# The prologue of an AdaLN-FFN block kernel: first products ahead of the second pairs' convolutions, W_up loaded earlier, half of agg_w in another buffer

## The chip, the cores and the metric

The kernel runs on one core of one Trainium2 chip. The metric is the time of one execution on the device, in microseconds (us); the median of three runs is what counts. TensorE (PE in the profile) multiplies, VectorE (DVE) and GpSimd (POOL) do elementwise work, ScalarE (ACT) copies and activations, and SyncE (SP) issues DMA transfers; DMAs can also be issued by ACT and POOL. Each engine works through its own instructions in the order in which the program gives them, and the order is written out by hand here.

## The reference

A batch of 128 samples with 64 channels of 1,024 values goes through two blocks, each of which adds its result to x:

```
# block 0: a per-sample channel mix, then a low-rank layer
att   = softmax(mlp(cond_128))                      # 128 x 8
agg_w = einsum('bk,koi->boi', att, weight); agg_b = att @ bias_k
y     = einsum('boi,bih->boh', agg_w, x) + agg_b[:, :, None]
x     = x + y @ (A @ B.T).T + bias                  # rank 128
# block 1: grouped convolution (9 taps, 4 groups), then a routed layer
y     = conv1d(x, weight, groups=4) + ctx + fside
base  = y @ W_up.T                                  # 1024 x 1024
one   = one_hot(argmax(y @ gate_w.T + expert_bias)) # 4 experts
delta = sum over e of one[e] * (y @ lora_A[e].T) @ lora_B[e].T
x     = x + base + delta
```

## The kernel before

**Tiling.** Two samples make a *pair*: a tile of 128 partitions (2 x 64 channels) by 1,024. There are 64 pairs, and two pairs, 2d and 2d+1, make a *group* d of the last layer, 32 groups in all.

**Block 0 for a pair.** `layer0_in` multiplies the transposed x by B into the PSUM tile pxb, and ScalarE copies it to xb. `layer0_mix` multiplies xb by the pair's agg_w (pz, then z: pairs 0 to 3 have theirs from `own_bd` and `own_bias`, which VectorE and ScalarE compute in the kernel; later pairs read it back from the DRAM tile aggd through `load_cond`). `layer0_out` multiplies z by A (pd, two halves), VectorE adds it to x, SP writes x to a DRAM tile x1d and reads it back in the order that the convolution needs into one of three SBUF tiles X (pair number modulo 3). The read waits until the write has landed. `add_fbias` adds the bias to x on VectorE or GpSimd.

**Convolution for a pair.** Pairs 0 and 1 use `conv`: products of X with the taps (pc, L429), evacuated by VectorE into the tile yt. From pair 2 on it takes `differences` (GpSimd reads X), `shared_in` (pm, L400), `shared_out`, `conv_in` (pc, L438) and `conv_out`.

**The last layer for a group.** W_up is held in quarters 11, 12, 21, 22 of 1 MB each, and the product takes seven half-size products instead of eight, with the weights T1 = 12 - 11, T2 = 22 - T1, T3 = 22 - 12 and -T4 = 21 - T2 (`w_sum`, VectorE, once) and with sums s0 to s3 of y (`ffn_sums`, GpSimd). A group does `gate_in`, `ffn_a` (product with 11), `ffn_second` (21), then `ffn`: gate, T2, T3, T1, the transposition `turn`, -T4, 22. VectorE and GpSimd add the intermediate results u2 and u3 to x on the way; `tiles` runs the next group's convolution beside the low-rank products (`lora`) and stores the results.

**Order.** Lines 624 to 714 are the prologue: conditions, pairs 0 to 3 through block 0, the convolutions of pairs 0 to 3, block 0 of pair 4 and parts of pair 5, the first two products of group 0. From line 715 a loop over the 32 groups repeats one order; its first pass still has the five other products of group 0. `tiles(0)` begins with `shared_in(4)`.

**Queues and buffers.** SP's queue in the prologue has, in this order: x of pair 3, x1d and X of pair 1, W_11, W_21, x1d of pair 2, x of pair 4, X of pair 2, W_12 (four pieces, in the buffers of s0 to s3), W_22, x1d of pair 3, aggb and the two halves of agg_w to DRAM (`agg_out`), X of pair 3, and `load_cond(2)`, whose read of aggd waits until agg_w has landed. x of pairs 5 to 7 is issued by GpSimd. The two halves of agg_w wait in SBUF in the buffers that become T3 (wT3) and -T4 (w-T4); so `w_sum` for T3 and -T4 cannot write before agg_w has been stored.

Of the kernel before, what the change touches and what calls it, by code (L numbers as in the profile page):

```python
# [35 lines left out]
F32 = mybir.dt.float32  # L36
AF = mybir.ActivationFunctionType
ALU = mybir.AluOpType
# [3 lines left out]
P = 128  # L42
NB, CH, L = 128, 64, 1024
NPAIR = NB // 2
# [24 lines left out]
def block(ctx: ExitStack, tc: tile.TileContext, a: dict, out: bass.AP):  # L69
# [58 lines left out]
    load_x(0, nc.sync)  # L128
    at = loaded("AT", [P, L])
    wk = loaded("wk", [P, 8, 2, CH], eng=nc.scalar)  # L130
    W, W12 = {}, []

    def load_w(name, eng):
        W[name] = const.tile([P, HC, N], F32, name=f"w{name}")
        eng.dma_start(W[name], a[f"w{name}"])

    def load_w12(eng):
        for c in range(HC):
            W12.append(sums.tile([P, N], F32, tag=f"s{c}", name=f"w12_{c}"))
            eng.dma_start(W12[c], a["w12"][:, c])  # L140

    def w_sum(name, x, y):
        W[name] = const.tile([P, HC, N], F32, tag=f"w{name}", name=f"w{name}")
        if "12" not in (x, y):
            nc.vector.tensor_tensor(W[name], W[x], W[y], ALU.subtract)
            return
        for c in range(HC):
            u, w = (W12[c] if n == "12" else W[n][:, c] for n in (x, y))
            nc.vector.tensor_tensor(W[name][:, c], u, w, ALU.subtract)


    X = []
# [147 lines left out]
    def agg_all():  # L300

        to = aggd.rearrange("b i o -> b (i o)").rearrange("b (j h n) -> h b j n", j=4, h=2)
        for h in range(2):
            agg = const.tile([NB, 4, 512], F32, tag=("wT3", "w-T4")[h], name=f"agg{h}")
            aggs.append((to[h], agg))
            ps4 = [spare(j, f"pagg{h}_{j}") for j in range(4)]
            for j in range(4):
                rows = slice(32 * j, 32 * (j + 1))
                nc.tensor.matmul(ps4[j], attT[rows, :], wa[rows, h], start=True, stop=True)
            for j in range(4):  # L310
                if j % 2:
                    nc.scalar.copy(agg[:, j], ps4[j])
                else:
                    nc.vector.tensor_copy(agg[:, j], ps4[j])
            yield
# [5 lines left out]

    lo, hi = slice(0, N), slice(N, L)
    xbs, z0s, yts, opened = {}, {}, {}, {}
    diffs, pms, m2s, pcs, zgs, vs, ss = {}, {}, {}, {}, {}, {}, {}

    def layer0_in(pr):
        xt = xts.pop(pr)
# [20 lines left out]
            nc.vector.scalar_tensor_tensor(to, aggbs[g][:, t], bsum, pzv, ALU.mult, ALU.add)  # L348
        z0s[pr] = z0

    def layer0_out(pr, then=None):
        x, z0 = xs[pr], z0s.pop(pr)
        xt = X[pr % NX]
        d = x1d.tile([Q, P, P], F32, tag="x1d", name=f"x1d{pr}")
        dv = d.rearrange("q (c g) m -> (q c) g m", g=BG)
        h = P // 2
        for hf in range(2):
            cols = slice(hf * 512, (hf + 1) * 512)
            qs = slice(hf * Q // 2, (hf + 1) * Q // 2)
            pd = bank(f"pd{pr}_{hf}")  # L360
            nc.tensor.matmul(pd, z0, at[:, cols], start=True, stop=True)  # L361
            nc.vector.tensor_tensor(x[:, cols], pd, x[:, cols], ALU.add)  # L362
            nc.sync.dma_start(
                d[qs].rearrange("q r m -> r q m"), x[:, cols].rearrange("r (q m) -> r q m", m=P)
            )
        if then:
            then()
        nc.sync.dma_start(xt[h:, :, :P], dv[:h])
        nc.sync.dma_start(xt[:h, :, 1 : P + 1], dv[h:])

    def blocks(pr, b, g, first):

# [96 lines left out]
    def halves(d):  # L469

        yt = yts[d]
        return [[yt[:, t, h * HC : (h + 1) * HC] for h in range(2)] for t in range(2)]
# [36 lines left out]
    def gate(d):  # L509

        zg = zgs.pop(d)
        pt = bank(f"pgt{d}")
        for t in range(2):
            nc.tensor.matmul(pt[:, t * GL : (t + 1) * GL], zg[:, t], fold, start=True, stop=True)  # L514
        pv = pt[:, : 2 * GL].rearrange("p (t c) -> p t c", t=2)
        lg = sp.tile([P, 2, E], F32, tag="lg", name=f"lg{d}")
        nc.vector.tensor_tensor(lg, pv[:, :, :E], ebias.unsqueeze(1).to_broadcast([P, 2, E]), ALU.add)
        mx = sp.tile([P, 2], F32, tag="mx", name=f"mx{d}")
        nc.vector.tensor_reduce(mx, lg, AX.X, ALU.max)
        sc = sp.tile([P, 2, E], F32, tag="sc", name=f"sc{d}")  # L520
        nc.vector.tensor_tensor(sc, lg, mx.unsqueeze(2).to_broadcast([P, 2, E]), ALU.is_equal)
        nc.vector.tensor_tensor(sc, sc, rank.unsqueeze(1).to_broadcast([P, 2, E]), ALU.mult)
        ms = sp.tile([P, 2], F32, tag="ms", name=f"ms{d}")
        nc.vector.tensor_reduce(ms, sc, AX.X, ALU.max)
        oh = sp.tile([P, 2, E], F32, tag="oh", name=f"oh{d}")
        nc.vector.tensor_tensor(oh, sc, ms.unsqueeze(2).to_broadcast([P, 2, E]), ALU.is_equal)
        zm = sp.tile([P, 2, 2, E, R], F32, tag="zm", name=f"zm{d}")
        for h in range(2):
            nc.vector.tensor_tensor(
                zm[:, :, h],  # L530
                pv[:, :, E:].rearrange("p t (e r) -> p t e r", e=E),
                oh.unsqueeze(3).to_broadcast([P, 2, E, R]),
                ALU.mult,
            )
        return zm
# [8 lines left out]
    def ffn_second(d):  # L544
        product(opened[d][0], halves(d)[0][1], W["21"], False)

    def ffn(d):

        b1 = halves(d)[1][1]
        p, v, s = opened[d], vs.pop(d), ss.pop(d)  # L550
        xa, xb = xs[2 * d], xs[2 * d + 1]
        zm = gate(d)
        product(p[1], s[1], W["T2"])
        u2 = sums.tile([P, N], F32, tag="u2", name=f"u2_{d}")
        nc.vector.tensor_tensor(u2, p[1], v, ALU.add)  # L555
        nc.gpsimd.tensor_tensor(xa[:, hi], xa[:, hi], u2, ALU.add)  # L556
        nc.gpsimd.tensor_tensor(xb[:, lo], xb[:, lo], u2, ALU.add)
        if 2 * d + 4 < NPAIR:
            differences(2 * d + 4)
        product(p[2], s[2], W["T3"])  # L560
        u3 = sums.tile([P, N], F32, tag="u3", name=f"u3_{d}")
        nc.vector.tensor_tensor(u3, p[2], u2, ALU.add)
        nc.gpsimd.tensor_tensor(xb[:, hi], xb[:, hi], u3, ALU.add)
        if 2 * d + 5 < NPAIR:
            differences(2 * d + 5)
        product(p[3], s[0], W["T1"])
        nc.vector.tensor_tensor(xb[:, hi], p[3], xb[:, hi], ALU.add)  # L567
        zt = turn(d, zm)
        product(p[2], b1, W["-T4"], False)
        product(p[3], s[3], W["22"], False)  # L570
        del yts[d]
        return zt

    def lora(d, zt):

# [82 lines left out]
    load_context(1)  # L658
    gl = loaded("gl", [P, NC, GT], eng=nc.scalar)
    lb = loaded("lb", [P, N], eng=nc.scalar)  # L660
    layer0_out(1)
    load_w("11", nc.sync)
    load_w("21", nc.sync)
    wsum = const.tile([P, NGC, P], F32, tag="sel", name="wsum")
    nc.gpsimd.tensor_tensor(wsum, ws[:, :, 0], ws[:, :, 1], ALU.add)
    add_fbias(3, nc.gpsimd)
    next(agg)
    own_bd(2)
    own_bias(2)
    layer0_in(2)  # L670
    conv(0)
    layer0_mix(2)
    layer0_out(2, lambda: load_x(4, nc.sync))
    own_bd(3)
    own_bias(3)
    load_w12(nc.sync)
    load_w("22", nc.sync)
    layer0_in(3)
    conv(1)
    layer0_mix(3)  # L680
    layer0_out(3, agg_out)
    add_fbias(4, nc.gpsimd)
    differences(2)
    gate_out(0, gate_in(0))
    ffn_a(0)
    w_sum("T1", "12", "11")
    w_sum("T2", "22", "T1")
    load_x(5)
    load_cond(2)
    layer0_in(4)  # L690
    differences(3)
    ffn_second(0)
    shared_in(2)
    shared_in(3)
    conv_in(2, 0)
    shared_out(2)
# [5 lines left out]
    conv_out(2, 1)  # L702
    conv_out(3, 0)
    conv_out(3, 1)
    add_fbias(5, nc.gpsimd)
    layer0_in(5)
    layer0_mix(4)
    w_sum("T3", "22", "12")
    w_sum("-T4", "21", "T2")
    ffn_sums(0)  # L710
    layer0_mix(5)
    layer0_out(4)
    load_x(6)
    load_x(7)
    for d in range(NPAIR // 2):
        more = d + 1 < NPAIR // 2
        ahead = [pr for pr in (2 * d + 6, 2 * d + 7) if pr < NPAIR]
        if 2 * d + 5 < NPAIR:
            layer0_out(2 * d + 5)
            load_context(d + 2)  # L720
        if ahead:
            load_cond(d + 3)
        for pr in ahead:
            add_fbias(pr, nc.gpsimd)
        tiles(d, ffn(d), 2 * d + 4, 2 * d + 5)
        for pr in (2 * d + 8, 2 * d + 9):
            if pr < NPAIR:
                load_x(pr)
        if more:
            ffn_sums(d + 1)  # L730
        for pr in ahead:
            layer0_in(pr)
        if ahead:
            layer0_mix(ahead[0])
        if more:
            ffn_a(d + 1)
        if ahead:
            layer0_out(ahead[0])
            layer0_mix(ahead[1])
        if more:  # L740
            ffn_second(d + 1)
# [104 lines left out]
```

## Time and profile before

| | us |
|---|---|
| median of 3 runs | 1358.75 (1358.67 to 1359.2) |
| the profiled execution, run time | 1359.87 |
| its span, first to last instruction | 1358.0 |
| TensorE busy | 1322.0 (97%) |
| GpSimd busy | 614.9 (45%) |
| VectorE busy | 555.3 (41%) |
| ScalarE busy | 139.2 (10%) |
| chain of work that ended last: TensorE / DMA / VectorE | 93% / 4% / 2% |
| one pass of the loop (start of `shared_in` at 113.39 and 153.82 on the chain) | 40.43 |

The profile is that of one execution. The chain is followed back from the last instruction, at each step to what released it. "busy" of TensorE is the time in which a matmul is under way. PEclk is the share of full speed that the chip granted to TensorE. In the view by stretches each row is a window of the span; the columns are its length, then for each engine busy time and number of instructions, the granted clock, the mean busy share of the 16 DMA engines, and GB/s.

### The profile page before, as it was taken

The numbers are of one execution on the slowest core, as the hardware profiler recorded it, in microseconds if no ns is written. First come the engines' busy times: TensorE is split into PE (matmuls) and PEld (weight loads), VectorE is DVE, ScalarE is ACT, GpSimd is POOL, SyncE is SP. The second block draws the span as 40 slices with busy tenths as digits, with TensorE's granted clock in tenths as the row PEclk, the third lists the DMA queues.
The fourth block names the chain that finished last, engine by engine and source line by source line (L and its number), as shares of the span: only waits on it lengthen the run. The fifth ranks groups of instructions, "written<-read, shape, count | busy, mean of one in ns | idle before, by whom it ended". The sixth has DMA issues, their size and how long they took to land.

```text
span 1358.0 us, 18275 instructions
## 1 busy us (share of the span) xinstructions
PE 1322.0 (97%) x7303; PEld 762.2 (56%) x7303; DVE 555.3 (41%) x984; ACT 139.2 (10%) x310; POOL 614.9 (45%) x547
## 2 busy tenths in 40 slices
PE   8679999999999999999999999999999999999997
PEld 6445555566555566555566555556555556655543
DVE  6453443444342444343444343344344344444222
ACT  2101100011101011111011111011111011110000
POOL 2155345544345544435553435553435554346321
PEclk9979999999999999999999999999999999999999
DMA  8934445553445544445544434554444555343301
GB/s 295 325 103 148 119 119 165 151 156 126 125 108 159 158 146 144 125 112 140 165 149 140 133 105 134 165 150 144 130 108 129 165 151 154 118 124 99 96 32 62
DMA packets 184276, 189.37 MB, mean 139 GB/s; under 512 B 17408, under 2 KB 156672, under 8 KB 183808
## 3 DMA queue, kind: packets, MB, share of 16 engines
q1 hardware_dynamic: 166048, 122.66, 32.5%
q0 software_dynamic: 16992, 61.87, 13.7%
q10 hardware_dynamic: 1152, 3.67, 0.8%
q8 instruction: 58, 0.95, 0.3%
q14 instruction: 26, 0.21, 0.1%
HBM read 118.90 MB, written 69.27 MB: 139 GB/s over the span
## 4 chain that ended last, share of the span: by engine, by line
PE 93%; DMA 4%; DVE 2%; issue 0%; ACT 0%; SPq 0%; DVEq 0%; ACTq 0%
PE pb L465 56%; PE pxb L330 8%; PE pc L438 8%; PE pd L361 8%; PE pm L400 4%; PE pg L496 4%; PE pb L580 2%; DMA x1d<-x 2%; DMA X<-x1d 1%; PE pz L340 1%; PE pgt L514 1%; DMA x<-in_x 1%; DMA xt<-in_xt 0%; PE pc L429 0%; PE pzt L539 0%
## 5 line engine op out<-in xcount | busy, mean ns | idle before, releaser
L465 PE MATMUL pb<-wT,s 128*128 128x512 f32 x768 | 337.5, 596 | 0.0
L109 POOL DMA_DIRECT2D x<-in_x x59 | 31.1, 528 | 503.5 <-DVE z L348 417.8
L465 PEld LDWEIGHTS pb<-wT,s 128*128 128x128 f32 x768 | 143.6, 190 | 168.4 <-issue 168.1
L465 PE MATMUL pb<-w,yt 128*128 128x512 f32 x512 | 230.8, 593 | 3.1 <-DVE x L586 1.7
L362 DVE TENSOR_TENSOR x<-pd,x 128x512 f32<-128x512 f32 x128 | 88.3, 691 | 233.0 <-PE pd L361 232.8
L415 DVE TENSOR_TENSOR m<-pm,cx 64x512 f32<-64x512 f32 x124 | 85.4, 689 | 228.6 <-PE pm L400 225.7
L591 POOL TENSOR_TENSOR x<-x,ffn_bias 128x1024 f32<-128x1024 f32 x62 | 144.7, 2355 | 47.4 <-DMA x<-in_x 47.4
L465 PEld LDWEIGHTS pb<-w,yt 128*128 128x128 f32 x512 | 92.4, 190 | 98.6 <-issue 92.2
L330 PEld LDWEIGHTS pxb<-B,xt 128*128 128x128 f32 x1024 | 118.8, 194 | 24.6 <-DVE yt L450 22.0
L361 PE MATMUL pd<-AT,z 128*128 128x512 f32 x256 | 122.9, 602 | 7.9 <-DVE z L348 6.1
L450 DVE TENSOR_TENSOR yt<-pc,m 128x512 f32<-128x512 f32 x124 | 121.4, 1098 | 21.7 <-ACT m L418 20.8
L330 PE MATMUL pxb<-B,xt 128*128 128x128 f32 x1024 | 125.0, 280 | 0.0
L465 PE MATMUL pb<-w,s 128*128 128x512 f32 x256 | 116.9, 600 | 2.1 <-DVE x L567 2.1
L438 PE MATMUL pc<-ws,df 128*64 128x128 f32 x1984 | 115.3, 275 | 0.0
L465 PE MATMUL pb<-w-T,yt 128*128 128x512 f32 x256 | 115.2, 592 | 0.0
L438 PEld LDWEIGHTS pc<-ws,df 128*64 128x64 f32 x1984 | 112.2, 139 | 4.3
L418 ACT COPY m<-m 64x512 f32<-64x512 f32 x124 | 76.5, 617 | 282.8 <-DVE m L415 279.4
L556 POOL TENSOR_TENSOR x<-x,u 128x512 f32<-128x512 f32 x32 | 40.4, 1264 | 140.9 <-DVE u L555 140.9
L361 PEld LDWEIGHTS pd<-AT,z 128*128 128x128 f32 x256 | 48.6, 192 | 68.5 <-issue 58.4
L465 PEld LDWEIGHTS pb<-w,s 128*128 128x128 f32 x256 | 49.1, 192 | 64.8 <-issue 61.9
L465 PEld LDWEIGHTS pb<-w-T,yt 128*128 128x128 f32 x256 | 46.1, 190 | 55.1 <-issue 55.1
L400 PEld LDWEIGHTS pm<-wsum,X 128*64 128x64 f32 x992 | 54.4, 140 | 36.6 <-issue 36.6
(110 smaller groups left out, 1139.4 us busy)
## 6 DMA issues: line engine op xcount, KB each, us to landing
x1d<-x SPq DMA_DIRECT2D x128, 256.0 KB, 3.5
X<-x1d SPq DMA_DIRECT2D x128, 256.0 KB, 4.0
out<-x SPq DMA_DIRECT2D x64, 512.0 KB, 2.6
xt<-in_xt POOLq DMA_DIRECT2D x59, 512.0 KB, 4.5
x<-in_x POOLq DMA_DIRECT2D x59, 512.0 KB, 4.3
cx<-ctxd SPq DMA_DIRECT2D x32, 128.0 KB, 4.3
ab<-aggbd SPq DMA_DIRECT2D x30, 128.0 KB, 3.2
w<-in_w SPq DMA_DIRECT2D x3, 1024.0 KB, 8.9
```

Source lines behind the costliest of these rows:

```text
L330: nc.tensor.matmul(pxb[:, :P], xt[:, c, :], bt[:, c, :], start=(c == 0), stop=(c == NC - 1))
L361: nc.tensor.matmul(pd, z0, at[:, cols], start=True, stop=True)
L362: nc.vector.tensor_tensor(x[:, cols], pd, x[:, cols], ALU.add)
L400: nc.tensor.matmul(pm[b * H : (b + 1) * H, g * P : (g + 1) * P], blocks(pr, b, g, 1), wsum[:, g], start=True, stop=True,)
L415: nc.vector.tensor_tensor(by_group(m2[half, b]), by_group(pm[half]), context(pr, b, half), ALU.add)
L418: nc.scalar.copy(m2[other, b], m2[half, b])
L438: nc.tensor.matmul(pc[o * H : (o + 1) * H, cols], diffs[pr][:, 2 * g + b, o], ws[:, g, o], start=True, stop=True,)
L450: nc.vector.tensor_tensor(yt.rearrange("m q (o g two) -> m two g q o", two=2, g=NGC)[:, b], by_group(pcs.pop((pr, b))), context(pr, b) if ...
L465: nc.tensor.matmul(to, yt[:, c], w[:, c], start=first and c == 0, stop=c == HC - 1, skip_group_check=not first)
L496: nc.tensor.matmul(pg[rows, : 2 * P].rearrange("m (t r) -> m t r", t=2), gl[:, c, :], yt[:, :, c], start=c < 2, stop=c >= NC - 2,)
L556: nc.gpsimd.tensor_tensor(xa[:, hi], xa[:, hi], u2, ALU.add)
L591: eng.tensor_tensor(xs[pr], xs[pr], fbias, ALU.add)
```

## The change

The prologue and the first pass of the loop are put in another order; nothing is computed differently.

- `ffn` is cut into `ffn_both` (T2), `ffn_b` (T3), `ffn_hi` (T1) and `ffn_last` (turn, -T4, 22), so that the prologue can issue the parts of group 0 between other work. `layer0_out` can hand back its X reads (`later=True`) so that they are issued later.
- The second half of agg_w waits in a buffer of the pool of yt instead of that of -T4; W_12 is loaded whole into the buffer of -T4 instead of in four pieces into those of s0 to s3.
- W_11, W_21, W_12 and W_22, x of pair 4 and `agg_out` are issued ahead of x1d of pairs 2 and 3. W_11 is even ahead of X of pair 1. `load_cond(2)` stands ahead of X of pair 2. x of pairs 5 to 7 moves from GpSimd's queue to SP's.
- Block 0 of pairs 2 and 3 stands ahead of the convolution of pair 1; all products of group 0 up to T1 stand ahead of the convolutions of pairs 2 and 3, with block 0 of pairs 4 and 5 between them. -T4 and 22 come after these convolutions.

```diff
-            agg = const.tile([NB, 4, 512], F32, tag=("wT3", "w-T4")[h], name=f"agg{h}")
+            pool, tag = ((const, "wT3"), (ytp, "yt"))[h]
+            agg = pool.tile([NB, 4, 512], F32, tag=tag, name=f"agg{h}")
...
+        def back():
+            nc.sync.dma_start(xt[h:, :, :P], dv[:h])
+            nc.sync.dma_start(xt[:h, :, 1 : P + 1], dv[h:])
+        if later:
+            return back
+        back()
...
+    def ffn_both(d):
+        xa, xb = xs[2 * d], xs[2 * d + 1]
+        product(opened[d][1], ss[d][1], W["T2"])
+        u2s[d] = sums.tile([P, N], F32, tag="u2", name=f"u2_{d}")
+        nc.vector.tensor_tensor(u2s[d], opened[d][1], vs.pop(d), ALU.add)
+        nc.gpsimd.tensor_tensor(xa[:, hi], xa[:, hi], u2s[d], ALU.add)
+        nc.gpsimd.tensor_tensor(xb[:, lo], xb[:, lo], u2s[d], ALU.add)
+    def ffn_b(d):
+        xb = xs[2 * d + 1]
+        product(opened[d][2], ss[d][2], W["T3"])
+        u3 = sums.tile([P, N], F32, tag="u3", name=f"u3_{d}")
+        nc.vector.tensor_tensor(u3, opened[d][2], u2s.pop(d), ALU.add)
+        nc.gpsimd.tensor_tensor(xb[:, hi], xb[:, hi], u3, ALU.add)
+    def ffn_hi(d):
+        xb = xs[2 * d + 1]
+        product(opened[d][3], ss[d][0], W["T1"])
+        nc.vector.tensor_tensor(xb[:, hi], opened[d][3], xb[:, hi], ALU.add)
+    def ffn_last(d, zm):
+        p, s = opened[d], ss.pop(d)
         zt = turn(d, zm)
-        product(p[2], b1, W["-T4"], False)
+        product(p[2], halves(d)[1][1], W["-T4"], False)
         product(p[3], s[3], W["22"], False)
...
-    layer0_out(1)
-    load_w("11", nc.sync)
+    layer0_out(1, lambda: load_w("11", nc.sync))
+    load_x(4, nc.sync)
     load_w("21", nc.sync)
+    load_w("12", nc.sync, tag="w-T4")
+    load_w("22", nc.sync)
...
     next(agg)
+    agg_out()
     own_bd(2)
     own_bias(2)
     layer0_in(2)
+    own_bd(3)
+    own_bias(3)
     conv(0)
     layer0_mix(2)
-    layer0_out(2, lambda: load_x(4, nc.sync))
-    own_bd(3)
-    own_bias(3)
-    load_w12(nc.sync)
-    load_w("22", nc.sync)
+    back2 = layer0_out(2, later=True)
     layer0_in(3)
+    layer0_mix(3)
+    back3 = layer0_out(3, later=True)
+    load_cond(2)
+    back2()
+    load_x(5, nc.sync)
+    back3()
     conv(1)
-    layer0_mix(3)
-    layer0_out(3, agg_out)
+
+    gate_out(0, gate_in(0))
+    ffn_sums(0)
     add_fbias(4, nc.gpsimd)
-    differences(2)
-    gate_out(0, gate_in(0))
     ffn_a(0)
+    layer0_in(4)
     w_sum("T1", "12", "11")
     w_sum("T2", "22", "T1")
-    load_x(5)
-    load_cond(2)
-    layer0_in(4)
+    w_sum("T3", "22", "12")
+    ffn_second(0)
+    zm = gate(0)
+    ffn_both(0)
+    ffn_b(0)
+    differences(2)
+    layer0_mix(4)
+    layer0_out(4, lambda: load_x(6, nc.sync))
+    w_sum("-T4", "21", "T2")
+    ffn_hi(0)
+    add_fbias(5, nc.gpsimd)
     differences(3)
-    ffn_second(0)
+    layer0_in(5)
+    layer0_mix(5)
+    back5 = layer0_out(5, lambda: load_x(7, nc.sync), later=True)
     shared_in(2)
+    back5()
     shared_in(3)
     conv_in(2, 0)
...
-    add_fbias(5, nc.gpsimd)
-    layer0_in(5)
-    layer0_mix(4)
-    w_sum("T3", "22", "12")
-    w_sum("-T4", "21", "T2")
-    ffn_sums(0)
-    layer0_mix(5)
-    layer0_out(4)
-    load_x(6)
-    load_x(7)
     for d in range(NPAIR // 2):
...
+        if d and 2 * d + 5 < NPAIR:
+            layer0_out(2 * d + 5)
         if 2 * d + 5 < NPAIR:
-            layer0_out(2 * d + 5)
             load_context(d + 2)
...
-        tiles(d, ffn(d), 2 * d + 4, 2 * d + 5)
+        if d:
+            zt = ffn(d)
+        else:
+            differences(4)
+            differences(5)
+            zt = ffn_last(0, zm)
+        tiles(d, zt, 2 * d + 4, 2 * d + 5)
```

More of the change, by code (lines that the diff above doesn't have):

```diff
@@ L130, in block, with load_w @@
     wk = loaded("wk", [P, 8, 2, CH], eng=nc.scalar)
-    W, W12 = {}, []
-    def load_w(name, eng):
-        W[name] = const.tile([P, HC, N], F32, name=f"w{name}")
+    W = {}
+    def load_w(name, eng, tag=None):
+        W[name] = const.tile([P, HC, N], F32, tag=tag or f"w{name}", name=f"w{name}")
         eng.dma_start(W[name], a[f"w{name}"])
[L137 to L140, printed above, removed]
     def w_sum(name, x, y):
         W[name] = const.tile([P, HC, N], F32, tag=f"w{name}", name=f"w{name}")
[L144 to L149, printed above, removed]
+        nc.vector.tensor_tensor(W[name], W[x], W[y], ALU.subtract)
     X = []
@@ L323, in block @@
     xbs, z0s, yts, opened = {}, {}, {}, {}
-    diffs, pms, m2s, pcs, zgs, vs, ss = {}, {}, {}, {}, {}, {}, {}
+    diffs, pms, m2s, pcs, zgs, vs, ss, u2s = {}, {}, {}, {}, {}, {}, {}, {}
     def layer0_in(pr):
@@ L349, in layer0_mix, with layer0_out @@
         z0s[pr] = z0
-    def layer0_out(pr, then=None):
+    def layer0_out(pr, then=None, later=False):
         x, z0 = xs[pr], z0s.pop(pr)
@@ L367, in layer0_out @@
             then()
-        nc.sync.dma_start(xt[h:, :, :P], dv[:h])
-        nc.sync.dma_start(xt[:h, :, 1 : P + 1], dv[h:])
+        def back():
[4 more added lines that the diff above has]
+        back()
     def blocks(pr, b, g, first):
@@ L545, in ffn_second @@
         product(opened[d][0], halves(d)[0][1], W["21"], False)
-    def ffn(d):
-        b1 = halves(d)[1][1]
-        p, v, s = opened[d], vs.pop(d), ss.pop(d)
+    def ffn_both(d):
         xa, xb = xs[2 * d], xs[2 * d + 1]
[L552 to L560, printed above, removed]
+        product(opened[d][1], ss[d][1], W["T2"])
[6 more added lines that the diff above has]
+        product(opened[d][2], ss[d][2], W["T3"])
         u3 = sums.tile([P, N], F32, tag="u3", name=f"u3_{d}")
-        nc.vector.tensor_tensor(u3, p[2], u2, ALU.add)
+        nc.vector.tensor_tensor(u3, opened[d][2], u2s.pop(d), ALU.add)
         nc.gpsimd.tensor_tensor(xb[:, hi], xb[:, hi], u3, ALU.add)
[L564 to L567, printed above, removed]
+    def ffn_hi(d):
[4 more added lines that the diff above has]
+        p, s = opened[d], ss.pop(d)
         zt = turn(d, zm)
-        product(p[2], b1, W["-T4"], False)
+        product(p[2], halves(d)[1][1], W["-T4"], False)
         product(p[3], s[3], W["22"], False)
@@ L572, in ffn @@
         return zt
+    def ffn(d):
+        zm = gate(d)
+        ffn_both(d)
+        if 2 * d + 4 < NPAIR:
+            differences(2 * d + 4)
+        ffn_b(d)
+        if 2 * d + 5 < NPAIR:
+            differences(2 * d + 5)
+        ffn_hi(d)
+        return ffn_last(d, zm)
     def lora(d, zt):
```

## The prediction

> **What bounds the kernel now.** I read the page's strip of slices first: TensorE is near full everywhere except in the first four slices of 34 us each, and there alone the granted clock drops.
>
> ```profile
> PE   8679999999999999999999999999999999999997
> ...
> PEclk9979999999999999999999999999999999999999
> ```
>
> So the loop is TensorE's own work, which the change doesn't touch, and only the prologue has time to give. Next, what TensorE waited for in the first 140 us:
>
> ```profile
> PE pm L400 <- DMA X<-x1d: 12.8, 1, 12.8
> PE pd L361 <- DVE z L348: 6.1, 1, 6.1
> PE pb L465 <- DVE x L567: 2.1, 1, 2.1
> ```
>
> Three waits, 21.0 us. Then the view by stretches, cut at these waits (columns: length; busy time of PE, PEld, DVE, ACT, POOL; clock, DMA share, GB/s):
>
> ```profile
> 29.30:56.80 27.50, 26.61 (x224) 18.13 (x224) 14.97 (x24) 2.51 (x8) 8.35 (x6) 1.00 0.93 293
> 56.80:69.64 12.84, 0.00 (x1) 0.03 (x1) 4.05 (x4) 1.23 (x2) 0.00 (x0) 0.67 0.96 322
> 69.64:76.70 7.06, 7.06 (x81) 6.89 (x81) 4.08 (x5) 1.23 (x2) 4.36 (x3) 0.63 0.08 24
> ...
> 81.40:87.45 6.05, 0.00 (x1) 0.00 (x1) 6.05 (x5) 0.00 (x0) 5.97 (x4) 0.80 0.00 0
> 87.45:91.20 3.75, 3.75 (x6) 1.68 (x6) 1.83 (x3) 0.00 (x0) 2.90 (x5) 0.50 0.60 98
> ...
> 105.90:108.00 2.10, 0.01 (x1) 0.01 (x1) 0.69 (x1) 0.00 (x0) 1.31 (x2) 1.00 0.96 216
> 108.00:113.40 5.40, 5.40 (x10) 2.10 (x12) 0.00 (x0) 0.00 (x0) 2.55 (x3) 0.68 0.39 81
> 113.40:153.80 40.40, 40.40 (x227) 23.25 (x227) 16.24 (x29) 4.12 (x9) 19.41 (x17) 1.00 0.52 149
> ```
>
> To see: in the 12.84 us DMA is full (0.96) and all engines starve for X of pair 3; in the 6.05 us DMA is empty and VectorE is full, since z of pair 5 stands behind the sums T3 and -T4; after each of the three waits the clock is down, so the wait is paid again in part. Last the chain of waits, for the price of each step at full clock:
>
> ```profile
> 113.39 1.90 PE pm L400 x32
> 115.29 1.73 PE pg L496 x16
> 117.02 3.49 PE pc L438 x64
> ...
> 121.58 3.77 PE pxb L330 x32
> 125.35 0.22 PE pz L340 x2
> 125.57 3.44 PE pb L465 x8
> 129.01 1.72 PE pd L361 x4
> ```
>
> The first three are for two pairs together, pxb too; one product (pb) costs 3.44, one pair's pd 1.72.
>
> **What the Trainium skill says.** "TensorE: Matmul & The Clock Gate", Part 1: the clock halves after an idle window of about 3.4 us and comes back after about as long a busy one. The trace agrees on the halving (0.50 in the 2 us stretches from 62 to 74) and shows it after the 2.1 us wait too (0.50 at 110 to 112). "SBUF — State Buffer", "Who interferes with whom": a VectorE instruction with two SBUF inputs and a GpSimd instruction that reads SBUF exclude each other. The trace agrees: -T4 took 3.34 us beside s3 on GpSimd, which took 3.32, against 2.29 for T2 and 1.27 for an s sum undisturbed. "DMA: Bandwidth & Descriptors", "Issuing engines are not separate DMA queues": all queues share the 16 engines. So moving x of pairs 5 to 7 from GpSimd to SP gains no bandwidth; 0.93 and 0.96 above show none was free.
>
> **The change part by part.** I compare one point, the start of `shared_in(4)` in `tiles(0)`: 113.39 before. From there on both programs issue the same. Up to the convolution of pair 0 (29.3, when X of pair 0 has landed) they agree as well.
>
> *Work between the points.* The set of TensorE steps is the same in both. At full clock: seven products 24.1 (7 x 3.44); convolutions of pairs 0 and 1 7.4 (3.72 each, from the chain); of pairs 2 and 3 5.4 (1.90 + 3.49); pxb of pairs 3 to 5 5.7; pd of four pairs 6.9; pz 2.1 (0.85 for each of pairs 2 and 3, 0.22 for each of 4 and 5); gate and transposition 2.2. Sum 53.8. Before takes 113.39 - 29.3 = 84.1, so 30.3 are lost: 21.0 in the three waits, 6.0 to the half clock (pm and pc 7.06 instead of 5.39; pd of pair 5 3.78 instead of 1.72; gate 0.70 instead of 0.37; product 22 5.40 instead of 3.44), about 3.3 in small gaps.
>
> *After, in TensorE's order.* conv(0) to 33.0; pz, z by ScalarE (a gap of 0.4), pd to 35.9; `own_bd(3)` (2.96 of VectorE) now stands ahead of the evacuation of conv(0), which ends at 36.05, so pxb of pair 3 waits 0.1 for its bank; xb and z of pair 3 now have no convolution between them: gaps 0.45 and 0.4; pd to 41.9. conv(1) to 45.6; X of pair 1 landed at 37.96 before and now has W_11 ahead of it (1 MB, some 2.7 us at 390 GB/s): about 40.5, covered. `gate_in(0)` must wait for the last `conv_out` (1.1): 46.7 to 48.5. Product 11 to 51.9, pxb of pair 4 to 53.8, product 21 to 57.2, gate to 57.6, T2 to 61.0, T3 to 64.5, pz of pair 4, z behind u3 on VectorE (gap 0.75), pd to 67.2, T1 to 70.6, pxb of pair 5, xb and z (gaps 0.45 and 0.75), pd to 75.7, convolutions of pairs 2 and 3 to 81.1, transposition, -T4, 22 to 88.1. Gaps 4.4 in all; with 0.6 of rounding and small ones already in the trace, 53.8 + 4.4 + 0.6 gives 88.1 as the start of `shared_in(4)`.
>
> *Do the operands come in time?* VectorE from 46.7: T1, T2, T3 at 2.29, against s0 to s3 (1.27 each) and `add_fbias(4)` (2.35) on GpSimd; by the exclusion they alternate, 14.3 us: s1 and T2 by 54, needed at 57.6; s2 by 58, needed at 61; the last by 61, needed by pd's addition at 66. The sums T1 to T3 have behind them on VectorE the gate's small operations and u2, which nobody needs before 62. T3 also waits for the first half of agg_w to be stored, and the buffer of yt of group 1 for the second.
> DMA: after 33.4 (x1d of pair 1 landed) the queue has X of pair 1 (0.5 MB at some 255 GB/s, 2 us), x of pair 4 and the W quarters (6 MB at the 385 to 442 GB/s of the 2 us stretches 52 to 56, 15.5 us), agg_w (2 MB, 5.2): stored at M = 56; by the other way, 8.9 MB from 29.3 on (27.5 us x 293 and 10.6 us x 322 GB/s until the store landed at 67.4 before, less the 2.6 MB of x of pair 5, x1d of pairs 2 and 3 and X of pair 2 that now come later) at 293, M = 59.7. T3 then is done at 58 at most, needed at 61. `load_cond(2)` waits for M on SP with both X reads, x of pair 5 and all later issues behind it. Its ab landed 4.5 after the store before: 60.5, needed at 64.7. Behind it X of pair 2 lands at about 61.5, x of pair 5 at 65, X of pair 3 at 67, by the issue times of 0.5 to 0.6 each and 4 us to landing; needed at 77, 70.6 (pxb) and 77. The wait that was 12.8 us has 10 to spare. X of pair 4 (x1d written at 67, xt and x of pair 6 in front) lands at 77, X of pair 5 at 86; needed at 88 and 90. `add_fbias(6)`, `(7)` and both differences on GpSimd end at 89.6, needed at 91.8 by `conv_in(4, 0)`.
>
> *The other waits.* The 6.1 us go: z of pairs 4 and 5 has at most one sum ahead. -T4 may be held by the exclusion until 73.7 and hold z of pair 5 by 0.4. The 2.1 us go: GpSimd adds u3 ahead of any difference, so nothing late stands before x L567. The half clock goes with the waits: no gap is over 1.15.
>
> *Unknown costs.* Nothing in before shows this order of transfers. Lower bound 0 (all slacks hold; a gain beyond is excluded, since work is fixed, except that up to 2 of the 4.4 of gaps may be overlapped). Upper bound: M = 65, as if the 8.9 MB moved at 249 GB/s: z of pair 4 is 4.3 late and the clock halves for 4 us of work, 2 more: 6.3. I take 1.6 with the exclusion's 0.4 in it. So `shared_in(4)` at 89.7, a gain of 23.7. The profiled execution goes from 1359.87 (span 1358.0 and 1.9 around it) to 1336.2; the median of runs is 1.1 below that execution, so 1358.75 - 23.7 = 1335.0.
>
> **The rivals.** *Transfers still bind* (M at 62 to 66, or the loads slow the stores of x1d). For: DMA share 0.93 to 0.96 and no byte is saved. Against: the big demand for X moves from 56.8 to 77. Loss 4 to 8 more: 1338 to 1343. *The clock gate trips* on several gaps in one window. For: 0.50 followed a wait of 2.1. Against: 23 to 25 us, where TensorE was busy 1.05 of 2, stayed at 1.00. One or two trips at 2 each: 1337 to 1339. *Slower*: `load_cond(2)` on SP becomes the bound, since agg_w's store, the reads of X of pairs 2 and 3 and x of pair 5 now form one chain. Each us of M beyond 60.5 costs one; the gain of 23.7 is used up at M = 84. That needs the 8.9 MB to move at 163 GB/s, while the two long full stretches show 293 and 322. At M = 90 it would be 1365. *It doesn't do what it says*: a buffer or PSUM bank I overlooked holds one product behind the convolution, so that the order is kept in name only; then half of the 30 is lost again, to 1350 or, at worst, no change.
>
> **How the numbers follow.** Forecast 0.62 (1332 to 1338); transfers 0.16; clock 0.10; overlooked buffer 0.06, of which half is no change; slower 0.06. The forecast's own range, widened to transfers and clock, is 1331 to 1343, which leaves out the last two and a tail. About 0.2% (2.7 us) is what a measurement can tell from no change: faster 0.91, same 0.03, slower 0.06.
>
> **What would show it.** Right: `shared_in(4)` near 89.7; no TensorE wait over 1.5 us after 30; clock 1.00 from 30 on; the passes of the loop still 40.4. Wrong: a wait for `z L348` of pair 4 with ab's DMA behind it (M too late), a wait of product T3 on w_sum, slices of 0.50 clock, or a longer pass.

## The result, and the profile after

The median went from 1358.97 to 1336.11 us: a ratio of 0.9835, 95% interval [0.9818, 0.9852], 22.9 us less. The prediction said 1335.0. The profiled execution took 1338.59, 2.5 more than the three others (1335.84 to 1336.14); the first experiment is about that.

The page's strip of slices for the changed kernel:

```profile
PE   8899999999999999999999999999999999999997
...
PEclk9999999999999999999999999999999999999999
```

The first three slices of before stood at 8, 6 and 7 tenths; now they stand at 8, 8 and 9, and the one slice of low clock (7) is at 9. What TensorE waited for in the first 130 us (total, times, longest):

```profile
PE pd L352 <- DVE yt L447: 1.8, 1, 1.8
...
PE pd L352 <- DVE z L339: 1.3, 2, 0.8
...
PE pg L493 <- DVE yt L447: 1.2, 1, 1.2
PE pd L352 <- ACT z L337: 0.8, 2, 0.4
PE pz L331 <- ACT xb L323: 0.8, 2, 0.4
```

Before had 12.8, 6.1 and 2.1 at the head of this view. No wait for X is left, and none for z of pair 5 behind the sums; of the five kinds shown, the last four are the small gaps that the prediction listed (pg is the product of `gate_in`). X of pair 3 itself landed no earlier: at 70.4, against 69.5 before. What went is the wait, since TensorE has other work until 79.6. The view by stretches, cut at the one new wait and at the start of `shared_in(4)`, with the columns of the prediction:

```profile
29.04:35.14 6.10, 5.67 (x70) 4.36 (x70) 5.75 (x11) 0.81 (x4) 2.35 (x1) 1.00 1.04 382
35.14:36.95 1.81, 0.00 (x1) 0.01 (x1) 1.74 (x4) 0.00 (x0) 0.00 (x0) 0.98 1.21 186
36.95:45.12 8.17, 7.34 (x26) 4.57 (x26) 2.75 (x4) 0.54 (x2) 0.00 (x0) 0.79 1.06 357
45.12:92.15 47.03, 44.18 (x282) 26.51 (x281) 28.98 (x33) 4.22 (x9) 29.08 (x15) 1.00 0.85 244
92.15:132.55 40.40, 40.40 (x226) 23.31 (x225) 16.09 (x29) 4.12 (x9) 24.95 (x23) 1.00 0.51 152
```

`shared_in(4)` starts at 92.15, against 113.32 before (113.39 on the chain): 21.2 us earlier in this execution. From there to the end both take 1244.7 us (1336.8 - 92.15 and 1358.0 - 113.32), and a pass of the loop still takes 40.4. So the whole difference lies where the change is. DMA is still full up to 56 (a share of 0.98 or more in every 2 us from 30), but TensorE now works beside it: from 45.12 to 92.15 it stands idle for 2.85 us.

The wait of 1.8 and the low clock behind it were not in the prediction. VectorE's and GpSimd's order in that place:

```profile
31.20 4.71 DVE L267 SCALAR_TENSOR_TENSOR bdx<-wk,attx,bdx 128x128 f32<-128x128 f32 x7
35.83 1.99 DVE L447 TENSOR_TENSOR yt<-pc,cx 128x512 f32<-128x512 f32 x2
```

```profile
31.86 2.35 POOL L603 TENSOR_TENSOR x<-x,ffn_bias 128x1024 f32<-128x1024 f32 x1 [7.51 <-DMA x<-in_x]
```

The seven steps of `own_bd(3)` took 4.71 us; those of `own_bd(2)` just before took 2.68. The 2.03 more are about one bias addition (2.35) of GpSimd, which began when x of pair 3 landed. The evacuation of conv(0) (yt) stands behind `own_bd(3)`, and the second half of pd of pair 2 waits for it. Of the four signs of being right that the prediction named, two failed in this execution: a wait over 1.5 us, and a clock under 1.00 after 30.

### The profile page after: what moved, and what is told of

It reads as the page before. It is cut to its first block, busy times and chain, and to the rows that moved or that the text cites. A ratio compares the mean times of both kernels' runs of the same rounds, so it can differ in the third digit from the quotient of the medians.

```text
span 1336.8 us, 18273 instructions
## 1 busy us (share of the span) xinstructions
PE 1317.1 (99%) x7303; PEld 759.3 (57%) x7303; DVE 552.8 (41%) x978; ACT 139.0 (10%) x310; POOL 616.5 (46%) x541
## 4 chain that ended last, share of the span: by engine, by line
PE 96%; DVE 2%; DMA 1%; issue 0%; ACT 0%; SPq 0%; DVEq 0%; ACTq 0%
PE pb L462 58%; PE pxb L321 9%; PE pd L352 8%; PE pc L435 8%; PE pm L397 4%; PE pg L493 4%; PE pb L592 2%; PE pz L331 1%; PE pgt L511 1%; DMA x<-in_x 1%; DVE bdx L267 1%; DMA xt<-in_xt 0%; DVE yt L447 0%; PE pc L426 0%; PE pzt L536 0%
## 5 line engine op out<-in xcount | busy, mean ns | idle before, releaser
L462 PEld LDWEIGHTS pb<-w,yt 128*128 128x128 f32 x512 | 92.4, 190 | 98.6 <-issue 92.2
L550 POOL TENSOR_TENSOR x<-x,u 128x512 f32<-128x512 f32 x32 | 40.4, 1264 | 144.6 <-DVE u L549 144.6
L352 PEld LDWEIGHTS pd<-AT,z 128*128 128x128 f32 x256 | 48.2, 191 | 65.3 <-issue 57.4
```

What stands on the lines that cost most here:

```text
L462: nc.tensor.matmul(to, yt[:, c], w[:, c], start=first and c == 0, stop=c == HC - 1, skip_group_check=not first)
L550: nc.gpsimd.tensor_tensor(xa[:, hi], xa[:, hi], u2s[d], ALU.add)
```

## The experiments

**What repeats?** The changed kernel itself, once more.

> The changed kernel once more, to see what of its trace repeats. Theory (GpSimd's bias addition for pair 3 and VectorE's own_bd(3) collide by chance of timing, and the half clock that follows is the 2.5 us by which the first profiled run, 1338.6, lies above the other runs, 1336.1): the median is 1336.1 again, and if this profiled run is near 1336 its trace shows TensorE's wait for the evacuation of conv(0) without the slices of half clock behind it, or a shorter wait. Rival (the 2.5 us are the profiler's or the loop's): wait of 1.8 us and half clock are there again and the run is still near 1336.

1336.15 median (1335.93 to 1337.95), this time with the profiled execution at 1336.07. VectorE, then TensorE:

```profile
30.33 4.65 DVE L267 SCALAR_TENSOR_TENSOR bdx<-wk,attx,bdx 128x128 f32<-128x128 f32 x7
34.90 1.99 DVE L447 TENSOR_TENSOR yt<-pc,cx 128x512 f32<-128x512 f32 x2
```

```profile
36.02 1.13 PE L352 MATMUL pd<-AT,z 128*128 128x512 f32 x2 [1.30 <-DMA X<-x1d]
```

`own_bd(3)` again took 4.65 us, the wait was 1.3 instead of 1.8, the clock stayed at 1.00 from 32 to 44, and `shared_in(4)` began at 89.59. (This view names a DMA as what ended the wait. The first half of the evacuation ended at 35.97, and pd began 0.05 behind it; in the first trace 0.06.) So the collision is in both traces and the half clock in one of them. Of the 2.56 us between 92.15 and 89.59 the half clock is 1.6 (pd 2.08 instead of 1.13, pxb 2.67 instead of 1.95), the longer wait 0.5, and conv(0), which began 0.4 later, the rest. The theory holds, but it put all 2.5 us down to the clock.

**Which of three parts carries the gain?** The change has an order of compute, an order of transfers, and other buffers. Four kernels undo or do parts. Each ratio is to the kernel before as it was measured beside that run (medians from 1358.67 to 1360.13), so the medians of different runs compare only to about 1 us.

> The kernel before with the new buffers alone: half of agg_w in the pool of yt, W_12 whole in the buffer of -T4 instead of in those of s0 to s3. Every order is that of before. Theory (the sums s0 to s3 on GpSimd no longer wait for T3, run ahead of it and no longer exclude T3 and -T4 on VectorE): T3 and -T4 take 4.6 us together instead of 8.0, z of pair 5 comes 3 us earlier, its wait falls from 6.1 to about 3, and with less half clock and the third wait gone the time is 1350 to 1354. Rival (buffers only allow the new order, they bring nothing themselves): 1357 to 1360.

```diff
-agg1 in "w-T4"; W_12 in four pieces in s0 to s3
+agg1 in the pool of yt; W_12 whole in "w-T4"      # all orders as before
```

1351.95 (1351.41 to 1352.97), ratio 0.9945 [0.9927, 0.9962]: the theory holds. VectorE before, then VectorE and GpSimd with the new buffers:

```profile
79.24 4.62 DVE L149 TENSOR_TENSOR wT<-w,w 128x512 f32<-128x512 f32 x4
83.79 3.34 DVE L145 TENSOR_TENSOR w-T<-w,wT 128x2048 f32<-128x2048 f32 x1
87.06 0.34 DVE L348 SCALAR_TENSOR_TENSOR z<-ab,bsum,pz 128x128 f32<-128x128 f32 x1
```

```profile
78.57 2.93 DVE L139 TENSOR_TENSOR wT<-w,w 128x2048 f32<-128x2048 f32 x1
81.54 2.29 DVE L139 TENSOR_TENSOR w-T<-w,wT 128x2048 f32<-128x2048 f32 x1
83.75 0.34 DVE L339 SCALAR_TENSOR_TENSOR z<-ab,bsum,pz 128x128 f32<-128x128 f32 x1
```

```profile
74.26 1.27 POOL L481 TENSOR_TENSOR s<-yt 128x512 f32<-128x512 f32 x1
75.61 1.28 POOL L482 TENSOR_TENSOR s<-s,yt 128x512 f32<-128x512 f32 x1
76.84 1.28 POOL L483 TENSOR_TENSOR s<-yt 128x512 f32<-128x512 f32 x1
78.07 1.28 POOL L484 TENSOR_TENSOR s<-yt,s 128x512 f32<-128x512 f32 x1
```

GpSimd's four sums no longer wait for T3 to free their buffers. They are over 0.8 us after the sums of W start (79.35 and 78.57), so T3 and -T4 take 5.2 us instead of 8.0, against 4.6 in the theory. TensorE's wait for z of pair 5 fell from 6.1 to 3.4 us, and the third wait, 2.1, is not there. That the buffers of s0 to s3 are the ones that matter is read from this trace; the two buffers were not changed one at a time.

> Undoes the order of compute alone: W loads, agg_out and load_cond(2) ahead of x1d and X of pairs 2 and 3 and the new buffers, with the convolutions of pairs 2 and 3 ahead of the products as before. Theory (X of pair 3 lands near 70 in either order, and only other work in front of its reader helps): TensorE waits 12 to 14 us for X of pair 3 again, and the two other waits stand: 1357 to 1363. Rival (earlier loads and freed buffers bring a part by themselves): 1353 or less.

```diff
 loads, agg_out, load_cond(2) and buffers as changed
-new order of compute: pairs 2 and 3 through block 0, products of group 0, then convolutions
+order of compute of before: conv(1), convolutions of pairs 2 and 3, then the products
```

1351.54 (1350.61 to 1352.14), ratio 0.9945 [0.9930, 0.9959]. My range, 1357 to 1363, is missed, and the rival's side is right: a part comes without the new order. But it comes from the buffers: buffers_only has the same ratio without the new transfers. What the new transfers did to the wait, in TensorE's order (start, length, idle before):

```profile
40.76 6.58 PE L426 MATMUL pc<-ws,X 128*64 128x128 f32 x64 [3.27 <-DMA X<-x1d]
...
64.63 1.98 PE L397 MATMUL pm<-wsum,X 128*64 128x128 f32 x16 [3.32 <-DMA X<-x1d]
69.77 1.97 PE L397 MATMUL pm<-wsum,X 128*64 128x128 f32 x16 [3.17 <-DMA X<-x1d]
```

The one wait of 13.0 for X of pair 3 (in buffers_only) became three, 9.8 in all, for X of pairs 1, 2 and 3, and conv(1) ran at half clock (6.58 instead of 3.72). In this order of compute the transfers only move the wait: the medians of the two kernels, 0.4 apart, cannot be told from each other.

> Undoes the order of the transfers alone: the new order of compute, with W_12 and W_22, x of pair 4, agg_out and the X reads on SP where they stood before. Theory (the order of compute carries the gain, the transfers have slack): agg_w is stored at about 67 instead of 56, so ab for z of pair 4 lands near 72 instead of 61 and is needed at 68.7: a wait of 3 to 4 us, with half clock behind it 5 to 8 in all: 1341 to 1344. Rival (the early W loads carry the gain): T2 and T3 come so late that more than half of the 23 us is lost: 1348 or more.

```diff
 new order of compute and new buffers
-W_11 to W_22, x of pair 4, agg_out, load_cond(2), then X of pairs 2 and 3
+W_11, W_21, x1d 2, x of pair 4, X 2, W_12, W_22, x1d 3, agg_out, X 3, load_cond(2)
```

1343.17 (1340.15 to 1343.83), ratio 0.9879 [0.9862, 0.9897], within the theory's range. VectorE's line for z of pair 4 (it needs ab, the rows of agg_b that `load_cond` reads), and TensorE's pd and T1 behind it:

```profile
72.28 0.35 DVE L339 SCALAR_TENSOR_TENSOR z<-ab,bsum,pz 128x128 f32<-128x128 f32 x1 [1.96 <-DMA ab<-aggbd]
```

```profile
72.69 3.14 PE L352 MATMUL pd<-AT,z 128*128 128x512 f32 x4 [2.87 <-DVE z L339]
75.62 4.18 PE L462 MATMUL pb<-wT,s 128*128 128x512 f32 x8
```

agg_w was stored at 65.2 instead of 55.8, ab landed at 72.2, and pd waited 2.87 and ran in part at half clock. In the medians the order of transfers is worth 7.0 us with the new order of compute (1343.17 - 1336.15). Not all of that need come from late data. In this trace the collision at `own_bd(3)` is there as well, and larger:

```profile
36.73 2.07 PE L352 MATMUL pd<-AT,z 128*128 128x512 f32 x2 [2.24 <-DVE yt L447]
38.60 3.62 PE L321 MATMUL pxb<-B,xt 128*128 128x128 f32 x16
```

From the start of conv(0) to that of conv(1) it took 17.5 us, against 13.9 in after_again: 3.5 more, the collision with its half clock. From conv(1) to `shared_in(4)` it took 51.5 against 47.0: 4.5 more, which is what the later data cost here. The profiled execution, at 1343.83, is the slowest of the four; whether the others had the larger collision too, and whether the order of transfers makes it, stays open. So the order of transfers is worth 4.5 to 7 us. Without the larger collision the time would lie near 1340, just under the theory's range, so part of that hit is luck.

> The changed kernel with the buffers of before: half of agg_w where -T4 comes, W_12 in four pieces in the buffers of s0 to s3, and therefore ffn_sums behind T3. Orders and transfers stay as changed. Theory (the buffers bring 7 us where T3 stands late, but in the new order T3 is summed by 58 and the sums are wanted from 61): s1 is ready by 59 and the time is 1335 to 1338. Rival (the buffers are needed in the new order as well, s1 and s2 are late for T2 and T3): a wait of 2 to 6 us at T2, 1339 to 1344.

1336.99 (1335.82 to 1337.69), ratio 0.9836 [0.9823, 0.9849], against 0.9836 [0.9818, 0.9854] for after_again: no loss that can be told, and T2 doesn't wait. GpSimd's s1, then TensorE's T2 and T3:

```profile
56.20 1.59 POOL L492 TENSOR_TENSOR s<-s,yt 128x512 f32<-128x512 f32 x1
```

```profile
59.25 7.11 PE L472 MATMUL pb<-wT,s 128*128 128x512 f32 x16
```

s1 was done at 57.8, 1.5 ahead of T2. With both new orders the buffers are no longer needed; they are worth 7 to 8 us where T3 stands late.

| kernel | compute | transfers | buffers | median us | ratio to before |
|---|---|---|---|---|---|
| buffers_only | old | old | new | 1351.95 | 0.9945 |
| old_order | old | new | new | 1351.54 | 0.9945 |
| old_loads | new | old | new | 1343.17 | 0.9879 |
| old_buffers | new | new | old | 1336.99 | 0.9836 |
| changed | new | new | new | 1336.11 | 0.9835 |

No part carries the gain alone. With the old order of compute the buffers bring 7 to 8 us and the new transfers nothing that can be told. With the new order of compute and the new buffers 15.5 us are gained even with the old transfers (1358.67 - 1343.17), and the new transfers add the rest. Not run: the new order of compute with both the old transfers and the old buffers. In old_loads x of pairs 5 to 7 stays on SP, so that move alone wasn't tested either.

**Do the three waits of before add up?**

> The kernel before, with the new buffers (half of agg_w in the pool of yt, W_12 whole in the buffer of -T4) and one move: the sums T3 and -T4 behind z of pair 5 on VectorE, ffn_sums ahead of it. If the three waits add up independently, the 6.1 us and some 2 of half clock go: 1351. Rival, which I hold likelier: the time comes back in the third wait, since TensorE then reaches x L567 earlier, while GpSimd stands there behind the differences of pair 4, whose X lands no earlier (its additions on VectorE stay behind the sums): that wait grows from 2.1 to 7 to 9 us and the time is 1356 to 1359.

```diff
+    ffn_sums(0)
+    layer0_mix(5)
     w_sum("T3", "22", "12")
     w_sum("-T4", "21", "T2")
-    ffn_sums(0)
-    layer0_mix(5)
     layer0_out(4)        # on the kernel before with the new buffers
```

1349.41, but scattered (1346.36 to 1353.45), ratio 0.9931 [0.9906, 0.9957]; my likelier rival is wrong. VectorE, then TensorE, in the profiled execution (the fastest, 1346.36):

```profile
76.99 2.28 DVE L139 TENSOR_TENSOR wT<-w,w 128x2048 f32<-128x2048 f32 x1
79.31 2.29 DVE L139 TENSOR_TENSOR w-T<-w,wT 128x2048 f32<-128x2048 f32 x1
```

```profile
82.26 0.64 PE L511 MATMUL pgt<-fold,zg 128*128 128x36 f32 x4 [2.10 <-DVE x L353]
```

The rival had the additions of pair 4 late behind the sums. Without GpSimd beside them T3 and -T4 took 4.6 us (76.99 to 81.6) instead of the 8.0 of before, so these additions came early enough for X of pair 4, and the third wait is not there. A wait of 2.1 for the additions stands at the gate instead. So in this execution the 6.1 us wait is gone and 2.1 comes back; what scatters the others was not traced. Whether it beats buffers_only isn't shown: the two intervals overlap.

**The new wait.** Two kernels take it apart: the order on VectorE, and the exclusion alone.

> The changed kernel with own_bd(3) behind conv(0) in VectorE's order instead of ahead of it. Theory (own_bd(3), stretched from 2.7 to 4.7 us by GpSimd's bias addition for pair 3, holds back the evacuation of conv(0)): TensorE's wait of 1.3 to 1.8 us before the second pd of pair 2 goes, and the clock stays at 1.00 from 36 to 40: 1334 to 1335 in the median against 1336.1, and the runs near 1338 disappear. Rival (own_bd(3) is then late for pz of pair 3): a new wait of 1 to 2 us at pz, 1336.

```diff
-    own_bd(3)
     own_bias(3)
     conv(0)
+    own_bd(3)
```

> The changed kernel in VectorE's own order, with own_bd(3) still ahead of conv(0)'s evacuation, but GpSimd's bias addition for pair 3 held until that evacuation, by a one-column addition that reads yt. It takes away the exclusion alone. Theory (GpSimd stretches own_bd(3)): own_bd(3) takes 2.7 us, not 4.7, the wait before the second pd of pair 2 and the half clock go, 1334 to 1335 as in bd3_behind_conv. Rival (the order on VectorE is what costs): own_bd(3) still delays the evacuation by 2 us, 1336.

```diff
     conv(0)
+    nc.gpsimd.tensor_tensor(nudge, y0, y0, ALU.add)   # y0: one column of yt
+    add_fbias(3, nc.gpsimd)                           # was ahead of next(agg)
```

VectorE and GpSimd in fbias3_later, then TensorE in bd3_behind_conv:

```profile
30.45 2.68 DVE L267 SCALAR_TENSOR_TENSOR bdx<-wk,attx,bdx 128x128 f32<-128x128 f32 x7
33.04 2.01 DVE L447 TENSOR_TENSOR yt<-pc,cx 128x512 f32<-128x512 f32 x2
```

```profile
34.34 2.36 POOL L603 TENSOR_TENSOR x<-x,ffn_bias 128x1024 f32<-128x1024 f32 x1
```

```profile
33.71 1.98 PE L352 MATMUL pd<-AT,z 128*128 128x512 f32 x4 [0.42 <-ACT z L337]
35.53 1.95 PE L321 MATMUL pxb<-B,xt 128*128 128x128 f32 x16
```

With the bias addition held back `own_bd(3)` is at 2.68 again, in the same order, and the wait is gone; with the order turned it is gone as well, and no new one appears at pz. `shared_in(4)` began at 88.04 (fbias3_later) and 88.15 (bd3_behind_conv), 1.4 to 1.6 ahead of after_again. Medians: 1335.24 (1334.53 to 1336.09), ratio 0.9824 [0.9811, 0.9838], and 1334.42 (1333.74 to 1334.78), ratio 0.9814 [0.9797, 0.9831]. None of the four executions of bd3_behind_conv stands out, as two of the eight of the changed kernel did (1338.59 and 1337.95, the others 1335.84 to 1336.23). The intervals of both overlap that of the changed kernel, so the gain in time isn't shown; that the exclusion makes the wait is shown by the traces.

**How much room have the transfers?**

> The changed kernel with four copies of 1 MB from DRAM to DRAM put on SP ahead of agg_out, to see how much room the transfers have. They need 4.2 MB read and 4.2 written, 11 to 20 us of the DMA engines. Theory (z of pair 4 has 7.7 us of room, T3 about 6, X of pair 3 about 6): all beyond some 7 us is lost, so 1340 to 1352, with waits for T3's sum, for ab and for X. Rival (transfers are hidden more deeply, by the order of the queue): 1338 or less; rival (transfers bind already): the whole 11 to 20 us is lost, 1347 to 1358.

> As ballast4 with two copies of 1 MB instead of four. Four made agg_w's first half land 10.9 us later and cost 6.1. Theory (T3's sum has about 5 to 6 us of room, all else more): two make it land 5.5 later and cost at most 1: 1336 to 1337. Rival (each us of transfer costs about half a us from the first on): 1339.

```diff
+    nc.sync.dma_start(spill0, a["w11"])    # 1 MB from DRAM to DRAM, two or four of them
     agg_out()
```

Four copies: 1342.20 (1341.70 to 1342.74), ratio 0.9871 [0.9850, 0.9891]. Two: 1336.41 (1335.74 to 1336.70), ratio 0.9832 [0.9818, 0.9845], no loss. T3's sum with two and with four copies:

```profile
57.14 4.44 DVE L139 TENSOR_TENSOR wT<-w,w 128x2048 f32<-128x2048 f32 x1 [3.61 <-DMA aggd<-agg]
```

```profile
64.23 2.29 DVE L139 TENSOR_TENSOR wT<-w,w 128x2048 f32<-128x2048 f32 x1 [9.48 <-DMA aggd<-agg]
```

TensorE's product T3 with four:

```profile
66.67 5.37 PE L462 MATMUL pb<-wT,s 128*128 128x512 f32 x8 [2.58 <-DVE lg L514]
```

The first half of agg_w landed at 57.0 and 64.1 instead of 53.3 (51.6 in after_again). With two, VectorE waits 3.6 us for it and product T3 doesn't; X of pair 3 lands at 74.9 and is not waited for either. With four, product T3 waits 2.6 us for its sum, done at 66.5, and then runs at half clock (5.37 instead of 3.44); ab, at 71.8, comes 0.9 ahead of its use. So a store 3.8 us later than in the first trace is free, and one 10.9 later costs 6.1 in the median. In the profiled execution `shared_in(4)` began 6.5 behind after_again; 4.5 of that is T3's wait with its half clock, and the other 2 are the collision at `own_bd(3)`, which here too had half clock behind it. Since T3 waits 2.6 of the 10.9, the room is between 4 and about 8 us counted from the first trace, and T3's sum is what runs out first.

**Can the listed gaps be filled?**

> As bd3_behind_conv, and other work in the four gaps that the prediction listed: pxb of pair 4 ahead of gate_in(0), pz of pair 4 ahead of T3, pxb of pair 5 ahead of T1, shared_in(2) ahead of pd of pair 5. Theory: the gaps of 1.18, 0.82, 0.41 and 0.44 us go, 2.8 in all, on top of bd3_behind_conv: 1331 to 1332. Rival (VectorE's and GpSimd's order moves the wait to the next step, for example T2 or X of pair 4): no better than bd3_behind_conv.

```diff
     conv(1)
+    layer0_in(4)
     gate_out(0, gate_in(0))
...
     ffn_both(0)
+    layer0_mix(4)
     ffn_b(0)
...
+    layer0_in(5)
     ffn_hi(0)
...
     layer0_mix(5)
+    shared_in(2)
     back5 = layer0_out(5, ..., later=True)
     # each + line stood a few lines further down and is taken out there
```

1333.10 (1332.25 to 1334.41), ratio 0.9806 [0.9788, 0.9824]. `shared_in(4)` began at 86.70, 1.45 before that of bd3_behind_conv instead of 2.8; conv(0) had begun 0.5 later here (29.28 and 28.74). TensorE and GpSimd:

```profile
53.55 3.70 PE L462 MATMUL pb<-w,yt 128*128 128x512 f32 x8 [0.68 <-ACT v L476]
...
90.23 4.17 PE L435 MATMUL pc<-ws,df 128*64 128x128 f32 x64
```

```profile
86.03 2.36 POOL L603 TENSOR_TENSOR x<-x,ffn_bias 128x1024 f32<-128x1024 f32 x1 [8.46 <-DMA x<-in_x]
88.35 1.04 POOL L389 TENSOR_TENSOR df<-X 128x512 f32<-128x512 f32 x1
```

pxb of pair 4 used to stand between products 11 and 21 and covered ScalarE's copy v; moved away, it leaves a wait of 0.68. And the convolution of pair 4 now comes 0.5 us short of the differences, which stand behind the bias addition for pair 7, which waits for x.

> From bd3_behind_conv: pxb of pair 3 between pz and pd of pair 2, conv(1) between pz and pd of pair 3, pz of pair 4 ahead of T3, pxb of pair 5 ahead of T1, shared_in(2) ahead of pd of pair 5, and in GpSimd's order the differences of pairs 4 and 5 ahead of the bias addition for pair 7, which waits for its x. gaps_filled reached 1333.1, with a wait of 0.7 new at product 21 and 0.5 lost behind the differences. Theory: the gaps of 0.4, 0.4, 0.4 and 1.2 us before 50, the 0.7 and the 0.5 go: 1330 to 1331.5. Rival (conv(1) ahead of pd of pair 3 waits for X of pair 1, which lands near 40): 1333.

```diff
     layer0_mix(2)
-    back2 = layer0_out(2, later=True)
     layer0_in(3)
+    back2 = layer0_out(2, later=True)
     layer0_mix(3)
+    conv(1)                               # stood behind back3()
     back3 = layer0_out(3, later=True)
...
     add_fbias(6); differences(4); differences(5); add_fbias(7)   # first pass
     # layer0_mix(4), layer0_in(5) and shared_in(2) as in gaps_filled
```

TensorE:

```profile
39.03 3.72 PE L426 MATMUL pc<-ws,X 128*64 128x128 f32 x64 [1.65 <-DMA X<-x1d]
```

The profiled execution took 1331.31, with `shared_in(4)` at 84.84, but conv(1) waited 1.65 us for X of pair 1 and the other runs took 1333.03 to 1337.32: median 1334.13, ratio 0.9821 [0.9808, 0.9835]. It isn't shown to be better than gaps_filled. conv(1) now depends on a transfer without any room; that this makes the spread was not traced. The best version with little spread is bd3_behind_conv, the lowest median gaps_filled; the intervals of these two overlap.

## Why the prediction was right

**Common work and what was lost before.** Right: from `shared_in(4)` on, 1244.7 us in both, and no wait of before is left. The forecast gain was 23.7 us; the medians give 22.9. The sum without unknown costs gave 88.1 for the start of `shared_in(4)`; the two kernels without the collision began it at 88.04 and 88.15. A little of that match is luck: conv(0) began at 28.64 and 28.74 in them, not at 29.3, so the work from there on took 59.4 instead of 58.8.

**The small gaps.** Listed 0.4, 0.45, 0.4, 1.1, 0.75, 0.45, 0.75; measured 0.42, 0.41, 0.42, 1.18, 0.82, 0.41, 0.44. -T4 did not hold z of pair 5.

**The term that was mis-sized** is `own_bd(3)`, "2.96 of VectorE", with a gap of 0.1 at pxb of pair 3. It took 5.0 (0.28 + 4.71) in the profiled execution, because GpSimd's bias addition for pair 3 runs in the same place: the exclusion that the prediction counted for T1 to T3 and s0 to s3 it did not count here. The gap came one step earlier, at the second half of pd of pair 2, and was 1.3 to 1.8 instead of 0.1, in one of the two traces with half clock behind it. Counted from conv(0) and against bd3_behind_conv, the collision cost 1.6 us in after_again and 3.7 in the first trace. The 1.6 set aside for unknown costs was meant for late transfers, with 0.4 in it for -T4; neither cost anything, and the collision took their place. That the start of `shared_in(4)` was forecast at 89.7 and measured at 89.59 in after_again is therefore luck. The 1.1 us by which the median is off come from the last step: the prediction put the median 1.1 under the profiled execution, as it was before, while after_again's profiled execution (1336.07) is at the median.

**Transfers.** The store of agg_w was put at 56 and landed at 55.8, ab at 60.5 and 61.0. Two errors cancel in that 56. Its sum has 6 MB for x of pair 4 and the four quarters of W_up; they are 5.2 (4 x 1,024 KB and 2 x 512 KB). And it has them at 385 to 442 GB/s, while the whole stretch from 33.4 to 55.8 ran at 363. Behind it the "4 us to landing" were too few: X of pair 2 landed at 65.3 (predicted 61.5), X of pair 3 at 70.4 (67), X of pair 4 at 81.1 (77), X of pair 5 at 92.2 (86). Only the room kept this from costing anything. It was least for x of pair 7, which landed at 90.6: GpSimd's bias addition waited for it, and the differences of pair 4 behind that ended at 95.1, 0.6 ahead of the convolution (95.7). The prediction had all four steps of GpSimd done by 89.6, 2.2 ahead. In gaps_filled, where TensorE came earlier, this is what cost 0.5.

**The sums.** T1 to T3, s0 to s3 and the bias addition alternate as forecast: 13.5 us (49.8 to 63.3) against 14.3, T3 done at 58.6 and used at 64.5.

**A reading of the strip.** The prediction says that the first four slices are low; the line shows three (8, 6, 7), and the fourth is at 9. Nothing rests on it.

**The rivals.** "Transfers still bind" is refuted by ballast2 for up to 3.8 us. "The clock gate trips" came true in one of the two traces, at 1.6 us, from a wait the prediction did not have. No overlooked buffer kept the old order: product T1 began at 70.99, and `shared_in(2)` behind it at 79.63. `load_cond(2)` on SP would have become the bound only with a store beyond 60.5; old_loads, with the store at 65.2, shows that the mechanism is real: its z of pair 4 waited for ab.

**What the prediction did not see** is how much the buffers matter by themselves: 7 to 8 us in the old order, nothing that can be told in the new.

## What to carry to other kernels

A wait for data goes away when independent work is put ahead of its reader; bringing other transfers forward only pays when the order of compute gives them something to feed (nothing that can be told against 4.5 to 7 us here). When a VectorE step is moved, look at what GpSimd does in the new place, not only in the old one, and check each buffer that two engines share for a false order between them.

## What was not expected of the hardware

- The exclusion between VectorE and GpSimd, which the prediction quotes for any VectorE instruction with two SBUF inputs and used for TENSOR_TENSOR only, showed for SCALAR_TENSOR_TENSOR on 128x128 as well: seven steps with all inputs in SBUF took 4.71 us beside a bias addition of 2.35, and 2.68 without.
- A wait of 1.8 us, with a gap of 0.42 ending 1.1 us before it, was followed by a clock of 0.50 from 37 to 40; so was one of 1.5 in the same place (ballast4), and one of 1.3 (after_again) was not. "TensorE: Matmul & The Clock Gate", Part 1, in the Trainium skill names an idle window of about 3.4 us; in these traces a shorter wait was enough. The length alone does not decide it: 1.65 us before conv(1) in gaps_filled2 and 2.10 at the gate in sums_behind_z were followed by 1.00, while 2.10 in the kernel before was followed by 0.50.
- Transfers of 512 KB that landed 4.1 to 4.5 us after issue in the median of the loop (x and xt) took 7 to 9 in the queue behind the store (xt and x of pair 5: issued at 59.2 and 59.8, landed at 66.6 and 69.0).
